# A two-layer graph network on one core: filter taps loaded before x and scaled a part ahead, a rearranged beginning, and other moved steps

## The chip, the cores and the metric

The kernel runs on one core of a Trainium2 chip. A core has a matrix engine (TensorE, PE in the profile, with its weight loads as PEld), a vector engine (VectorE, DVE), an activation engine (ScalarE, ACT), a general engine (GpSimd, POOL) and a queue engine that only issues transfers (SyncE, SP). ACT and POOL issue transfers too. Each engine takes its instructions in the order in which they stand in its own queue, and semaphores order the engines among each other. The metric is the device time of one execution in microseconds, and the median over the runs is compared.

## What is computed

There are 64 graphs of 256 nodes with 256 features each, and an adjacency matrix for each graph, all in float32. Layer 0 is a normalised graph convolution with residual and layer norm; layer 1 has a convolution branch, a message branch and a GRU gate.

```python
# layer 0
deg = adj.sum(-1); d = where(deg != 0, deg, 1) ** -0.5
h = (d[:, :, None] * adj * d[:, None, :] + alpha * eye) @ x
x = layernorm(x + h @ W.T + b)
# layer 1
h = relu(bn1(conv1d(x.T, conv1_w)))             # width 1
h = bn2(conv1d(h, conv2_w, pad=8))              # width 17
x_conv = relu(h + x.T).T
s = x @ w_se.T + b_se                           # 3 columns
A = exp(-(|s_n|^2 + |s_m|^2 - 2 s_n.s_m)) * adj # 256 x 256
x_nmp = A @ relu(x @ w_msg.T + b_msg)
gi = concat(x_conv, x_nmp) @ w_ih.T + b_ih; gh = x @ w_hh.T + b_hh
r, z = sigmoid(gi_r + gh_r), sigmoid(gi_z + gh_z)
x = layernorm(x + (1 - z) * tanh(gi_n + r * gh_n) + z * x)
```

## The kernel before, in words

The graphs go in four quarters of 16 (Q). The convolution of width 17 is done in a frequency domain of 48 points: each graph's hidden rows are transformed by a matrix (`p_dft`, L496), the transforms of a quarter are gathered in the tile `V`, multiplied there with the transformed filter (`p_k`, L559), and transformed back on DVE in small steps (`real_transform`, `complex_begin`, `complex_end`), in place in the same tile, called `VM` or `M`.

**Setup** (L1053 to L1108). Weights, vectors and first graphs are loaded. `tables` (L215) writes cosine rows on one partition (`period`, `fwd_row`, `w_row`) with many small DVE copies and spreads them by transfers into `fwd` and `wt`. `batch_norms` (L165) turns the batch norm vectors into factors: on DVE and POOL, then broadcast over the partitions by six matmuls with diagonal matrices (`p_norm`, L187), then multiplied into the weight tile `wc1` of the first convolution.

**The filter** comes in 13 parts. `load_taps` (L275) loads a part with seven transfers on SP (L291 to L293) into one of two buffers. `weights` (L295) has DVE scale the part (L300), makes 16 matmul records of it (`p_u`, L308), copies them to `u_set` (L311), forms a difference on DVE (L313) and a sum on POOL (L314), and writes three tiles to memory (L316). In the first quarter each of the first 13 graphs has one part beside it.

**A graph** passes through two generators. `layer0(g)` (L353): row sums on ACT (L363), their power on POOL (L373), alpha times the sums on DVE (`adeg`, L375), transposed adjacency and diagonal (L384 to L390), x scaled (L402, ACT), b0 added to x on POOL (L403), `p_hT` (L410), `p_out` (L420), scaling and residual on DVE (L425), then `layernorm` (L319): statistics on DVE, power on POOL (L329), `ln_mr` on DVE (L332), normalising on ACT (L334), and a store. `layer1(g)` (L444): `p_conv` (L457), squares of the three columns on DVE (L467 to L470), `p_msg`, `p_dft`, `p_rows` (L509), `p_dist` with the exponential on ACT (L521), the product with the adjacency on DVE (`aT`, L524), `p_nmp` (L533).

`graphs` (L1021) interleaves them: while graph i is in `layer1`, graph i+2 is in `layer0`, graph i+3 has its sums taken, and the loads of i+3 are issued. `PLACES` (L1012) says after which of the seven pieces of `layer1` a step of `layer0` or of the other work (a filter part in the first quarter) is put. The order inside an engine's queue is made by a planner ahead of the run, which takes ready instructions in the order of the program; `tc.issue_after(op)` makes the instructions in its block that run on op's engine stand behind op. `load` (L104) puts both loads of a graph on SP; the x tile has two buffers, and one comes free when L425 of the graph two before has read it. In `layer0`, the end of the layer norm (`ENDS`, L1029) was put behind the squares and the eviction of `p_conv`.

**Later quarters.** The frequency products run in 12 steps (L1171); in the first quarter each step also takes three pieces of the next graphs (`begin`). After that the GRU (`gru`, L877; `p_g`, L893) of one quarter runs beside the graphs of the next. The last quarter's GRU runs alone, and its last graph ends with the code at L935 to L965.

Of the kernel before, what the change touches and what calls it, by code (L numbers as in the profile page):

```python
# [9 lines left out]
F32 = mybir.dt.float32  # L10
# [16 lines left out]
def kernel(  # L27
# [76 lines left out]
    def load(g):  # L104
        if g >= B:
            return
        ain[g] = loads.tile([P, NCH, N], F32, name="adj_t")
        nc.sync.dma_start(ain[g], adj[g].rearrange("(c p) m -> p c m", p=P))
        xin[g] = loads.tile([P, NCH, D], F32, name="x_t")
        nc.sync.dma_start(xin[g], x[g].rearrange("(c p) f -> p c f", p=P))  # L110

# [15 lines left out]
    nc.scalar.copy(warm, neg_half)  # L127
    for i, a in enumerate((bn1_g, bn2_g, bn1_b, bn2_b, bn1_m, bn2_m, bn1_v, bn2_v)):
        (nc.sync if i % 2 else nc.scalar).dma_start(vectors[2 * i : 2 * i + 2], a.rearrange("(c p) -> c p", p=P))
    nc.scalar.dma_start(w0, w0T.rearrange("(k p) o -> p k o", p=P))  # L130
    load(1)
# [33 lines left out]
    def batch_norms(pool):  # L165
# [10 lines left out]
        nc.vector.tensor_mul(g, g, v)  # L176
        nc.vector.tensor_mul(m, m, g)
        nc.vector.tensor_sub(b, b, m)
        nc.vector.tensor_copy(bn2_bias, b[:, 2:4])

        ones = pool.tile([P, P], F32, name="ones")
        nc.vector.memset(ones, 1.0)
        rows = [bank("p_norm") for _ in range(2)]
        for i, col in enumerate((g[:, 0:1], g[:, 1:2], b[:, 0:1], b[:, 1:2], g[:, 2:3], g[:, 3:4])):
            diagonal = pool.tile([P, P], F32, name="diagonal", bufs=2)
            nc.vector.tensor_scalar(diagonal, ident, col, None, op0=ALU.mult)
            nc.tensor.matmul(rows[i // 4][:, i % 4 * P : (i % 4 + 1) * P], ones, diagonal, start=True, stop=True)  # L187
# [4 lines left out]
        nc.vector.tensor_copy(wc1[0:1, 0, :D], rows[0][0:1, D:])  # L192
# [22 lines left out]
    def tables(pool):  # L215
# [12 lines left out]
        nc.gpsimd.memset(fwd, 0.0)  # L228
        for r in range(2):
            nc.vector.memset(fwd_row[:, :, 2 * r], 1.0)  # L230
# [9 lines left out]
        with tc.issue_after(DIAGONAL[0]):  # L240

            for r in range(2):
                nc.vector.memset(w_row[:, :, r, NF], (0.5, 1.0)[r])
# [7 lines left out]
        for j in range(GT // 2 + 2):  # L251

            first = NT * (j - 1) - PAD
            lo, hi = max(first, 0), min(first + FL, P)
            nc.sync.dma_start(fwd[lo:hi, j, :], fwd_row[:, lo - first : hi - first])

# [16 lines left out]
    TAPS_OF = {}  # L273

    def load_taps(pool, n):  # L275
# [17 lines left out]
        nc.sync.dma_start(tp[KT - 1 :], taps(GC - 1, TR, 1, 1))  # L293

    def weights(pool, n, scale):  # L295
# [4 lines left out]
        nc.vector.tensor_mul(tp, tp, scale[:KT].unsqueeze(1).to_broadcast([KT, ng, D]))  # L300
# [3 lines left out]
        for i in range(2):  # L304
# [7 lines left out]
            if i == 1:  # L312
                nc.vector.tensor_sub(us[3], us[1], us[0])  # L313
                nc.gpsimd.tensor_tensor(us[2], us[0], us[1], op=ALU.add)  # L314
                for d, u in zip(ud, (us[0], us[3], us[2])):
                    nc.gpsimd.dma_start(d[:, n * ng : (n + 1) * ng], u)  # L316
            yield

    def layernorm(y, eps=LN_EPS, normed=None):  # L319

        chunks = range(y.shape[1])
        st = small.tile([P, NCH, nc.vector.BN_STATS_DIM], F32, name="ln_st")
        mv = small.tile([P, NCH, nc.vector.BN_AGGR_DIM], F32, name="ln_mv")
        rs = small.tile([P, NCH], F32, name="ln_rs")
        for c in chunks:
            nc.vector.bn_stats(st[:, c, :], y[:, c, :])
            nc.vector.bn_aggr(mv[:, c, :], st[:, c, :])
        nc.vector.tensor_scalar(rs[:, : len(chunks)], mv[:, : len(chunks), 1], eps, None, op0=ALU.add)  # L328
# [3 lines left out]
        nc.vector.scalar_tensor_tensor(mr[:, : len(chunks)], mv[:, : len(chunks), 0], -1.0, rs[:, : len(chunks)], op0=ALU.mult, op1=ALU.mult)  # L332
# [16 lines left out]
    EVICTED, RELU, SQUARED, AGGREGATED, LAYER0 = {}, {}, {}, {}, {}  # L349
    ADJT, X1, X_SCALED, DIAGONAL = {}, {}, {}, {}  # L350


    def layer0(g):  # L353
# [19 lines left out]
        nc.gpsimd.tensor_tensor(dis, deg, neg_half[:, :NCH], op=ALU.pow)  # L373
        adeg = small.tile([P, NCH], F32, name="adeg")
        nc.vector.tensor_scalar(adeg, deg, alpha_t, None, op0=ALU.mult)  # L375
# [27 lines left out]
        nc.gpsimd.tensor_tensor(x_t, x_t, b0_t.unsqueeze(1).to_broadcast([P, NCH, D]), op=ALU.add)  # L403

        yield
        hT = work.tile([P, DCH, N], F32, name="hT", bufs=1)
# [23 lines left out]
        yield from layernorm(x1, normed=NORMED)  # L430
# [437 lines left out]
    def normed(g, part, y):  # L868

        yield from layernorm(y, 4 * LN_EPS)  # L870
        nc.scalar.dma_start(out[g].rearrange("(c p) d -> p c d", p=P)[:, part], y)
# [5 lines left out]
    def gru(g):  # L877
# [57 lines left out]
        def squashed(c):  # L935
            rz = G[:, c, :, GR : GZ + 1, :].rearrange("p h t d -> p h (t d)")
            nc.scalar.activation(rz, rz, AF.Tanh, scale=0.5)  # L937

        squashed(1)

        def finished(part):
            both = G[:, part].rearrange("p c h t d -> p (c h) t d")
            chunks = both.shape[1] // 2
            r, z, n, i = (both[:, :, j, :] for j in (GR, GZ, GN, GI))
            nc.vector.scalar_tensor_tensor(n, r, 1.0, n, op0=ALU.add, op1=ALU.mult)
            i4 = i.rearrange("p (c h) d -> p c h d", h=2)
            bias = bn_t.rearrange("p (h d) -> p h d", h=2).unsqueeze(1).to_broadcast([P, chunks, 2, HD])
            nc.vector.tensor_tensor(i4, i4, bias, op=ALU.add)
# [10 lines left out]
        if g == B - 1:  # L959
            finished(slice(1, 2))  # L960
            ended()
# [298 lines left out]
```

## Time and profile before

| what | us |
|---|---|
| median of 3 runs (2070.37 to 2078.38) | 2074.39 |
| the profiled execution's own time | 2077.37 |
| its span | 2075.6 |
| PE busy | 1993.8 |
| DVE busy | 1360.7 |
| first `p_conv` | 34.10 |
| transposes of graph 2, of graph 12 (`p_x1T`) | 66.49, 244.27 |
| first frequency products of the first quarter | about 299.9 |
| end of the last matmul | 2064.1 |

The profile is of one execution. A row of the groups or waits names the source line, the engine, and the tiles as output<-input. A wait is written as "who <- whom: total, times, longest". The chain of work is followed back from the last instruction; each row has a start, a duration and the engine with its tile and line. "SPq" is SP's queue. The granted clock is the share of full speed that TensorE had. Times count from the span's start.

### The profile page before, as it was taken

The page shows a single profiled execution, that of the slowest core. Times are in us where ns is not written, and L with a number is a line of the kernel's source. Part 1 is how long each engine was busy: PE and PEld are TensorE (multiplying, and loading weights), DVE is VectorE, ACT ScalarE, POOL GpSimd, SP SyncE. Part 2 cuts the span into 40 slices and gives each one's busy share as a digit, 9 for nine tenths or more (in the row PEclk, how much of TensorE's full clock was granted, in tenths as well). Part 3 has the DMA queues.
Part 4 walks back from the last instruction along what each step waited for, and adds up shares of the span by engine and source line. Part 5 has one row for each costly group of instructions (what it writes and reads, how often), then busy time and mean ns, then how long its engine had stood idle before and what let it go on. Part 6 is the DMA issues. An engine that isn't in the chain of part 4 may idle for free.

```text
span 2075.6 us, 26338 instructions
## 1 busy us (share of the span) xinstructions
PE 1993.8 (96%) x8157; PEld 1445.7 (70%) x8157; DVE 1360.7 (66%) x3192; ACT 972.6 (47%) x2283; POOL 663.4 (32%) x672
## 2 busy tenths in 40 slices
PE   6989999999999999999999999999999999999997
PEld 5877788888667766777777766677767865555554
DVE  5434457587456788764455778775444899977776
ACT  3656664477442234556654223456655223333333
POOL 3433421022432234223332224323232034434442
PEclk9999999999999999999999999999999999999999
DMA  3765656544437655343334664434333944543431
GB/s 103 235 187 173 182 189 221 178 148 159 111 111 220 188 145 148 112 127 105 120 97 154 214 191 128 116 126 138 97 87 92 298 128 124 146 104 99 97 89 58
DMA packets 268936, 298.04 MB, mean 144 GB/s; under 512 B 84192, under 2 KB 211252, under 8 KB 268798
## 3 DMA queue, kind: packets, MB, share of 16 engines
q1 hardware_dynamic: 208846, 200.37, 33.2%
q10 hardware_dynamic: 44480, 67.39, 9.1%
q0 software_dynamic: 15472, 28.61, 6.4%
q8 instruction: 66, 1.08, 0.2%
q14 instruction: 72, 0.59, 0.1%
HBM read 193.19 MB, written 103.06 MB: 143 GB/s over the span
## 4 chain that ended last, share of the span: by engine, by line
PE 75%; DVE 12%; DMA 5%; ACT 3%; issue 2%; SPq 1%; POOL 1%; ACTq 0%; POOLq 0%; DVEq 0%
PE p_g L893 34%; PE p_k L559 10%; PE p_nmp L533 5%; PE p_hT L410 5%; PE p_out L420 4%; PE p_conv L457 4%; PE p_msg L478 3%; PE p_dft L496 3%; PE p_u L308 2%; PE p_dist L520 2%; PE p_x1T L440 1%; DMA u<-ud 1%; DMA taps<-in_conv2T_dram 1%; DMA inputs<-x_d 1%; PE p_adjT L384 1%
## 5 line engine op out<-in xcount | busy, mean ns | idle before, releaser
L893 PE MATMUL p_g<-wall,sums 128*128 128x384 f32 x1536 | 533.8, 488 | 2.8 <-DVE G L918 1.7
L893 PEld LDWEIGHTS p_g<-wall,sums 128*128 128x128 f32 x1536 | 284.9, 190 | 187.9 <-issue 9.5
L893 PE MATMUL p_g<-wall,inputs 128*128 128x384 f32 x1152 | 405.4, 487 | 6.9 <-DVE G L911 6.9
L893 PEld LDWEIGHTS p_g<-wall,inputs 128*128 128x128 f32 x1152 | 216.7, 190 | 157.4 <-DVE G L911 12.8
L864 POOL TENSOR_TENSOR sums<-inputs 128x384 f32<-128x384 f32 x128 | 141.8, 1108 | 332.3 <-PE p_g L893 309.5
L329 POOL TENSOR_TENSOR ln_rs<-ln_rs,neg_half 128x2 f32<-128x2 f32 x129 | 96.5, 748 | 458.7 <-DVE ln_rs L328 331.0
L524 DVE TENSOR_TENSOR aT<-aT,adjT 128x512 f32<-128x512 f32 x64 | 46.1, 720 | 253.5 <-ACT aT L521 253.5
L559 PE MATMUL p_k<-u,VM 128*128 128x256 f32 x736 | 171.3, 383 | 3.7 <-DMA u<-ud 2.4
L403 POOL TENSOR_TENSOR x_t<-x_t,b_t 128x512 f32<-128x512 f32 x64 | 89.1, 1392 | 249.4 <-ACT x L402 178.5
L559 PEld LDWEIGHTS p_k<-u,VM 128*128 128x128 f32 x736 | 139.6, 192 | 26.8 <-ACT ab L605 3.1
L410 PE MATMUL p_hT<-adjT,x 128*128 128x256 f32 x512 | 128.5, 396 | 13.3 <-ACT x L402 11.8
L533 PE MATMUL p_nmp<-aT,msg 128*128 128x256 f32 x512 | 125.3, 389 | 13.8 <-DVE aT L524 13.8
L937 ACT ACTIVATE G<-G 128x512 f32<-128x512 f32 x128 | 80.5, 631 | 123.7 <-DVE G L962 86.4
L334 ACT ACTIVATE x_g<-x_g,ln_mr,ln_rs 128x256 f32<-128x256 f32 x128 | 70.0, 593 | 137.8 <-DVE ln_mr L332 133.5
L420 PE MATMUL p_out<-w,hT 128*128 128x256 f32 x512 | 123.7, 385 | 7.8 <-ACT hT L415 7.6
L457 PE MATMUL p_conv<-wc,xn 128*128 128x259 f32 x512 | 124.6, 385 | 1.1 <-issue 1.1
L478 PE MATMUL p_msg<-wmsg,xn 128*128 128x256 f32 x512 | 121.3, 379 | 0.0
L533 PEld LDWEIGHTS p_nmp<-aT,msg 128*128 128x128 f32 x512 | 98.9, 194 | 30.7 <-DVE aT L524 16.9
L420 PEld LDWEIGHTS p_out<-w,hT 128*128 128x128 f32 x512 | 96.2, 192 | 30.8 <-ACT hT L415 13.8
L410 PEld LDWEIGHTS p_hT<-adjT,x 128*128 128x128 f32 x512 | 93.3, 195 | 34.5 <-ACT x L402 17.9
L864 POOL TENSOR_TENSOR sums<-inputs,sums 128x384 f32<-128x384 f32 x64 | 79.0, 1234 | 116.2 <-PE p_g L893 115.7
L496 PE MATMUL p_dft<-fwd,h 128*128 128x240 f32 x512 | 114.3, 366 | 0.0
(163 smaller groups left out, 3496.3 us busy)
## 6 DMA issues: line engine op xcount, KB each, us to landing
u<-ud SPq DMA_DIRECT2D x284, 256.0 KB
xn_d<-xn ACTq DMA_DIRECT2D x64, 512.0 KB
inputs<-xn_d SPq DMA_DIRECT2D x64, 512.0 KB
ud<-u_set POOLq DMA_DIRECT2D x39, 480.0 KB, 5.4
adj_t<-in_adj_dram SPq DMA_DIRECT2D x64, 256.0 KB
x_t<-in_x_dram SPq DMA_DIRECT2D x64, 256.0 KB
x_d<-x ACTq DMA_DIRECT2D x64, 256.0 KB
xc_d<-VM SPq DMA_DIRECT2D x64, 256.0 KB
```

Of the source, the lines that this page charges most:

```text
L329: nc.gpsimd.tensor_tensor(rs[:, : len(chunks)], rs[:, : len(chunks)], neg_half[:, : len(chunks)], op=ALU.pow)
L403: nc.gpsimd.tensor_tensor(x_t, x_t, b0_t.unsqueeze(1).to_broadcast([P, NCH, D]), op=ALU.add)
L410: nc.tensor.matmul(p[:, k, :], x1[:, mc, k * P : (k + 1) * P], adjT[:, mc, 1 - mc : 3 - mc, :].rearrange("p n q -> p (n q)"), start=mc == ...
L420: nc.tensor.matmul(p[:, c, :], hT[:, k, c * P : (c + 1) * P], w0[:, k, :], start=k == 0, stop=k == DCH - 1)
L457: nc.tensor.matmul(p, x1T[:, k, c * P : (c + 1) * P], wc1[:, k, :], start=k == 0, stop=k == DCH - 1)
L478: nc.tensor.matmul(p[:, c, :], x1T[:, k, c * P : (c + 1) * P], wmsg[:, k, :], start=k == 0, stop=k == DCH - 1)
L496: nc.tensor.matmul(p[:, t0 * FL : t1 * FL], h[:, c, k * P : (k + 1) * P], fwd[:, first : first + t1 - t0, :].rearrange("p t f -> p (t f)") ...
L533: nc.tensor.matmul(p[:, k, :], msg[:, mc, k * P : (k + 1) * P], aT[:, mc].rearrange("p n q -> p (n q)"), start=mc == 0, stop=mc == NCH - 1,)
L559: nc.tensor.matmul(p[:, j * D : (j + 1) * D], v[:, k, :], u[:, k, :], start=k == 0 and j == 0 and not onto, stop=k == DCH - 1, skip_group_ ...
L864: nc.gpsimd.tensor_tensor(S[i], x, y, op=op)
L893: nc.tensor.matmul(p[:, : 3 * HD] if k == 0 else p[:, HD:], a[:, k], wall[:, b, k].rearrange("p t d -> p (t d)"), start=first and k == 0, ...
L937: nc.scalar.activation(rz, rz, AF.Tanh, scale=0.5)
```

## The change

Nothing of what is computed is different. The parts:

- **Filter taps.** In the first quarter a graph's x load is put on SP behind the taps of the next part (before: with the adjacency load, ahead of them). The scaling of a part is done one part ahead, on DVE behind `aT` of the running graph. The difference, the sum and the three writes of a part are put behind `adeg` and the degrees' power of the graph three ahead. Part 0 starts one place later in graph 0.
- **Beginning.** The adjacency of graph 1 is loaded ahead of the batch norm vectors; of those, two are issued by ACT, three by POOL, three by SP. The cosine rows stand behind the second graph's diagonal, the rows for the filter behind the normalised `wc1`; the batch norm is cut in two pieces, whose matmuls come beside graph 1's `p_out`. Its diagonal matrices stand in `VM`. Two biases pass through a small tile.
- **Layer norm of layer 0.** `ln_mr` stands behind `adeg` of the next graph and is a piece of its own; the normalising on ACT waits for the eviction of `p_conv` alone. The b0 addition is a piece later.
- **Transform pieces** in the steps 4 to 11 of the first quarter stand on DVE behind the latest squares, diagonal and `aT` of the graphs.
- **The last graph** of all does the first half of the columns of its first 128 rows early, and takes the statistics of each half by itself.

```diff
+    def load_adj(g):
         ain[g] = loads.tile([P, NCH, N], F32, name="adj_t")
         nc.sync.dma_start(ain[g], adj[g].rearrange("(c p) m -> p c m", p=P))
+    def load_x(g):
         xin[g] = loads.tile([P, NCH, D], F32, name="x_t")
         nc.sync.dma_start(xin[g], x[g].rearrange("(c p) f -> p c f", p=P))
...
+    load_adj(1)
     for i, a in enumerate((bn1_g, bn2_g, bn1_b, bn2_b, bn1_m, bn2_m, bn1_v, bn2_v)):
-        (nc.sync if i % 2 else nc.scalar).dma_start(vectors[2 * i : 2 * i + 2], a.rearrange("(c p) -> c p", p=P))
+        (nc.scalar if i < 2 else nc.gpsimd if i < 5 else nc.sync).dma_start(
+            vectors[2 * i : 2 * i + 2], a.rearrange("(c p) -> c p", p=P)
+        )
+    load_x(1)
     nc.scalar.dma_start(w0, w0T.rearrange("(k p) o -> p k o", p=P))
-    load(1)
...
+        with tc.issue_after(DIAGONAL[1]):
+            nc.vector.tensor_mul(g, g, v)
...
+            for i, col in enumerate((g[:, 0:1], g[:, 1:2], b[:, 0:1], b[:, 1:2], g[:, 2:3], g[:, 3:4])):
+                nc.vector.tensor_scalar(VM[:, i, :P], ident, col, None, op0=ALU.mult)
+        yield
         rows = [bank("p_norm") for _ in range(2)]
...
-        nc.vector.tensor_copy(wc1[0:1, 0, :D], rows[0][0:1, D:])
+        NORMALISED.append(nc.vector.tensor_copy(wc1[0:1, 0, :D], rows[0][0:1, D:]).ins)
...
+        behind_diagonal = ExitStack()
+        behind_diagonal.enter_context(tc.issue_after(DIAGONAL[1]))
         for r in range(2):
             nc.vector.memset(fwd_row[:, :, 2 * r], 1.0)
...
-        with tc.issue_after(DIAGONAL[0]):
+        load_x(2)
+        yield
+        with tc.issue_after(NORMALISED[0]):
             for r in range(2):
                 nc.vector.memset(w_row[:, :, r, NF], (0.5, 1.0)[r])
...
+        TAPS_OF["last"] = nc.sync.dma_start(tp[KT - 1 :], taps(GC - 1, TR, 1, 1)).ins
+    def scaled(tp, scale):
+        nc.vector.tensor_mul(tp, tp, scale[:KT].unsqueeze(1).to_broadcast([KT, GW // NPARTS, D]))
...
-        nc.vector.tensor_mul(tp, tp, scale[:KT].unsqueeze(1).to_broadcast([KT, ng, D]))
+        if n == 0:
+            scaled(tp, scale)
...
+            if i == 1 and n + 1 < NPARTS:
+                with tc.issue_after(WEIGHED[n]):
+                    scaled(TAPS_OF[n + 1], scale)
+            yield
+        with tc.issue_after(ADEG[n + 3]), tc.issue_after(POWERS[n + 3]):
+            nc.vector.tensor_sub(us[3], us[1], us[0])
+            nc.gpsimd.tensor_tensor(us[2], us[0], us[1], op=ALU.add)
+            for d, u in zip(ud, (us[0], us[3], us[2])):
+                nc.gpsimd.dma_start(d[:, n * ng : (n + 1) * ng], u)
+        yield
...
+        with tc.issue_after(ADEG[first]) if first in ADEG else ExitStack():
+            nc.vector.scalar_tensor_tensor(mr[:, : len(chunks)], mv[:, : len(chunks), 0], -1.0, rs[:, : len(chunks)], op0=ALU.mult, op1=ALU.mult)
+        if normed is not None:
+            yield
...
+        yield
+        with tc.issue_after(POWERS[max(g, 1)]):
+            nc.gpsimd.tensor_tensor(x_t, x_t, b0_t.unsqueeze(1).to_broadcast([P, NCH, D]), op=ALU.add)
...
+        top = slice(0, 1)
+        squashed(0, top)
+        y = mixed(top, top)
+        st = small.tile([P, NCH, nc.vector.BN_STATS_DIM], F32, name="ln_st")
+        nc.vector.bn_stats(st[:, 0, :], y[:, 0, :HD])
+        squashed(1)
+        finished(slice(1, 2), mixed(slice(1, 2)))
+        nc.vector.tensor_add(quarter(0, 1), quarter(0, 1), p5)
+        squashed(0, slice(1, 2))
+        mixed(top, slice(1, 2))
+        nc.vector.bn_stats(st[:, 1, :], y[:, 0, HD:])
+        NORMS.append(normed(g, top, y, st))
+        ended()
...
-            load(first + i + 3)
+            if first:
+                load(first + i + 3)
+            else:
+                load_adj(i + 3)
...
-                    with tc.issue_after(EVICTED[first + i]), tc.issue_after(SQUARED[first + i]):
+                    with tc.issue_after(EVICTED[first + i]):
                         run(ENDS.pop())
...
                     next(of_layer0(first + i + 3), "end")
+                    next(given["layer0"], "end")
...
+                if piece == 0 and not first:
+                    with tc.issue_after(TAPS_OF["last"]):
+                        load_x(i + 3)
...
+        run(take(firsts[0], 2))
+        with tc.issue_after(STATISTICS[0]):
+            next(firsts[1])
+            scale2 = next(norms)
+        run(firsts[0])
+        run(fill)
+        next(firsts[1])
+        ENDS[0] = firsts[1]
...
+        others[0] = later(others[0])
...
+                if step >= 4:
+                    with ExitStack() as behind_graphs:
+                        for done in (SQUARED, DIAGONAL, WEIGHED):
+                            behind_graphs.enter_context(tc.issue_after(done[max(done)]))
+                        run(take(real, 1))
+                        run(complex_begin(step))
```

## The prediction

> **What bounds the kernel.** I read the page first, then busy time by stretch, then TensorE's waits, then the chain of work where they fall.
>
> ```profile
> span 2075.6 us, 26338 instructions
> PE 1993.8 (96%) x8157; PEld 1445.7 (70%) x8157; DVE 1360.7 (66%) x3192; ACT 972.6 (47%) x2283; POOL 663.4 (32%) x672
> ```
>
> TensorE (PE) is the bound. The change removes no matmul, so it can win only where PE stands idle (81.8 us in all) or runs at a reduced clock. By stretch (columns: length, busy time of PE, PEld, DVE, ACT, POOL; granted clock; DMA share; GB/s):
>
> ```profile
> 0.00:34.10 34.10, 17.18 (x57) 12.74 (x58) 21.04 (x142) 11.13 (x29) 11.34 (x21) 0.89 0.37 109
> ...
> 66.49:244.27 177.78, 163.47 (x781) 135.48 (x780) 76.62 (x178) 109.14 (x280) 68.97 (x71) 0.96 0.65 193
> ...
> 402.30:412.60 10.30, 8.15 (x25) 5.71 (x26) 4.96 (x9) 5.72 (x13) 1.26 (x1) 0.67 0.08 27
> ...
> 2064.10:2075.60 11.50, 0.01 (x1) 0.00 (x0) 5.50 (x19) 2.66 (x5) 1.32 (x2) 0.67 0.07 23
> ```
>
> Idle PE sits in four places: the beginning (first p_conv at 34.10), graphs 2 to 11 of the first sixteen (66.49 to 244.27), a spot at 402, and the tail after the last matmul. The change edits all four. Single graphs, from one p_x1T to the next:
>
> ```profile
> 99.44:120.26 20.82, 17.67 (x79) 14.27 (x78) 10.15 (x26) 10.84 (x28) 8.20 (x10) 0.89 0.78 224
> ...
> 174.77:193.85 19.08, 15.94 (x79) 13.10 (x78) 8.96 (x22) 10.84 (x28) 7.58 (x9) 1.00 0.65 190
> ...
> 228.60:244.27 15.67, 15.67 (x79) 13.18 (x78) 6.91 (x17) 10.84 (x28) 6.06 (x6) 1.00 0.61 187
> ```
>
> The same work takes 15.67 us when nothing stalls, 19.08 with one stall, 20.82 with a stall and a lowered clock. PE's waits before 300 us (total, times, longest), SP's own wait, and the chain through one stall:
>
> ```profile
> PE p_nmp L533 <- DVE aT L524: 13.0, 4, 3.5
> ...
> PE p_norm L187 <- DVE bn L178: 6.3, 1, 6.3
> ```
>
> ```profile
> SPq L110 <- DVE x L425: 54.4, 12, 11.9
> ```
>
> ```profile
> 101.26 0.39 SPq L110
> ...
> 101.69 2.53 SPq L291
> ...
> 104.26 2.98 SPq L291
> ...
> 107.28 6.25 DMA taps<-in_conv2T_dram
> ...
> 113.70 0.10 DVE taps L300
> ...
> 115.96 0.69 DVE aT L524
> ```
>
> SP holds the x load (L110) until L425 frees its buffer; five of the seven taps issues stand behind it. The taps land at 113.5. DVE has their scaling (L300) ahead of aT (L524), although the exponentials that aT needs were ready at about 112.1. So p_nmp starts at 116.69.
>
> **The change, part by part.** All sums are against the profiled execution: span 2075.6, time 2077.37, so 1.8 lies around the span. The median of the three runs is 2074.39; I take savings off that.
>
> **1. Taps before x, scaled a part ahead.** Nothing is removed: 13 scalings of 1.2 us, 91 issues and 13 sums remain. The x load moves behind the taps. Without it in between, the issues after 101.69 start 2.5 us earlier (99.18, where SP began to wait). The u_set sum and difference with three 480 KB writes move from before p_x1T (DVE 97.03, POOL 96.94) to behind adeg and the degrees' power of the graph three ahead (102.6 and 103.7). So the write burst follows the taps instead of meeting them, and L425 is no longer behind a difference that took 3.37 us. The scaling goes behind aT of the graph before the one that uses it. New wait: DVE may stand at L300 for late taps. Behind it would be L425, the statistics and next graph's squares (L467). With aT begun 12.7 us into a graph (96.42 against 83.76), and taps that even in the stalled graph landed 14.1 us in, less at least 2.5, they are there at about 11.6 or sooner. If that cover is gone, each late us above some 2 of DVE slack falls on p_rows. The x load itself: issued 101.26, first read by L402 at 129.92. A delay of some 4 us is covered. Adjacency and wall loads behind it on SP have a graph's slack as well.
>
> Size: graphs 2 to 11 took 177.78; ten at 15.67 are 156.7; the excess is 21.1. The waits proper are 13.0 + 1.3 (p_u on L300) = 14.3; the rest is clock. The Trainium skill (TensorE: Matmul & The Clock Gate, "What's actually happening") says that PE falls to half clock after an idle window of about 3.4 us. That speaks against counting the rest, since three of the four waits are 3.1 to 3.2. The rows decide: the graph with a 3.15 wait had clock 0.89 and took 1.74 longer than the one with 3.14. By the rule I would save about 14 plus one throttling (2); by the rows 21.1. I take 18.5, leaving 2.6 for denser DMA (193 GB/s becomes some 215; the freest stretch, 83.76 to 99.44, moved 259).
>
> **2. The beginning.** Removed: nothing but waits. Order moved: some 30 fwd_row copies (0.1 to 0.2 each) behind DIAGONAL[1], the w_row pieces (10.96 to 13.25) behind NORMALISED. Before, ACT had graph 1's row sums at 10.1, but DVE took them at 13.18, behind the w_row pieces: 3.1 late. Graph 0's diagonals waited from 7.9 to 10.40 behind the copies. Chain after, by these durations: the first sums 0.5 earlier, since ACT issues two bn loads instead of four and one of them waited 2.2; scaled x(0) at 8.4, p_hT(0) 8.4 to 11.8, p_hT(1) to 14.7 (2.94), p_out(0) to 16.6 (1.74), L425 and statistics to 18.6 (2.0), power 0.71, ln_mr and normalising to 20.8, transposes 0.6, two copies 0.9: first p_conv at 22.6. Meanwhile p_norm (3.12 at half clock, about 1.6 at full) runs after p_out(1) at about 19, and its product into wc1 (0.68 + 0.41) ends by 21.5. I add 1 for DVE beside POOL (L186 took 1.30 there against 0.28 alone): 23.6 instead of 34.1, so 10.5. Ends: 6 if the tables delay L425 and fwd; 12.5.
> The three bn loads on POOL cost 0.6 to 0.8 each (L1062, L1063), about 2, ahead of ident; the first adjacency lands only at 5.1, which covers them; uncovered, 2. The Trainium skill (DMA: Bandwidth & Descriptors, "Issuing engines are not separate DMA queues") says another issuing engine saves only issue time. By it adj_t(1) gains about 1; by the row (issued at 5.40 after a load issued at 1.76 had landed) 3.7. It matters little: graph 1's sums wait for x(0) on ACT anyway. I count only the 0.5. The two bias loads gain two POOL copies, not in the trace: nearest row a 1x256 memset, 0.30; ends 0.1 and 0.8; hidden.
>
> **3. Transform pieces behind the graphs' operations (steps 4 to 11 of the first quarter).**
>
> ```profile
> 402.18 0.33 DVE VM L614
> 402.51 0.08 DVE scols L470
> 402.59 0.07 DVE ln_mr L332
> ...
> 403.19 0.59 ACT x L334
> ...
> 404.86 2.94 PE p_hT L410 x8
> ```
>
> Transform pieces stood between L467 (399.43) and L470; PE lost 2.15 between 402.3 and 404.9, and the stretch's mean clock of 0.67 over 10.3 us means 6.8 us at half clock, costing 3.4: 5.5 in all. From 301.6 to 402.3 PE never waits, so there is nothing else to win. DVE there is busy 66 of 100.7, so pieces deferred have room. I take 4.5; ends 0 and 5.5.
>
> **4. ln_mr behind adeg, normalising a piece later.** Same instruction count. ACT's L334 stops waiting for squares and ln_mr (32.9 us over 30 graphs, on ACT). PE's share later on is 10.8 us of p_hT waiting for L402, which queues behind L334, and 2.4 of p_rows on ln_mr; the first 3.8 or so belong to part 3. Against: ln_mr now stands before the squares, so DVE waits out POOL's power. Between 411 and 515 the power ends 0.2 to 0.6 after the squares began; p_rows is later still on PE, so that is covered. Bounds -2 and 8; I take 3.5. The b0 addition on POOL (1.26 to 1.4) moves one piece later; L425 is 3 us or more behind it.
>
> **5. Tail.** The last matmul ends at 2064.1; then full-width pieces of 0.42 (128x256) and 0.63 run for the last chunk. Half of it is done earlier, with DVE idle between 2058.5 and 2060.3. Six pieces shrink by some 0.15 to 0.2 (1.0), and the second chunk's power no longer stands in front of the last difference (0.5), nor as much DVE work (0.5): 2.0; ends 0.5 and 3.
>
> Sum: 18.5 + 10.5 + 4.5 + 3.5 + 2.0 = 39.0; less 2.5 because graph 0 no longer has p_u as filler in its early pieces and the order shifts elsewhere: 36.5. 2074.4 - 36.5 = **2038**.
>
> **Rivals.** *Stalls only move (0.17):* scaling stands behind aT but taps are still late, and p_rows or p_u waits instead. For: DMA share already 0.65 to 0.85. Against: the 2.5 us and the moved burst. Part 1 gives 5: 2051. *The beginning is bound by loads and tables (0.12):* part 2 gives 3, by the fwd and wt transfers (28.48 to 33.8 for wt) or DVE order: 2045. *Everything works, clock included (0.09):* ends of 1 to 5 taken together (21 + 12.5 + 5.5 + 6 + 3): 2026. *Slower (0.04):* ln_mr blocks DVE in front of the squares wherever POOL's power queues behind the input sums (1.0 to 1.2 each). Over 48 later graphs this outweighs the gain from about 1 us a graph on PE; at 1.2 it costs 58 and gives 2096. In the trace the power ends at most 1.7 after adeg, and mostly 3 to 5 before the squares, so it is unlikely. *Unchanged (0.02).* The likeliest, 2030 to 2046, has the remaining 0.56.
>
> **Numbers.** 0.5% (10.4 us) is about what this kernel's measurement can tell from nothing. Above 2064 only the last two rivals: faster 0.94, same 0.02, slower 0.04. For 8 in 10 the range runs from the full gain to the half-failed part 1 with 3 for spread: 2025 to 2054.
>
> **What would show it.** First p_conv near 23.6; graphs 2 to 11 at 15.7 to 16 each with no p_nmp wait on aT and clock 1.00; no half clock near the first quarter's last steps; ln_mr before the squares; about 9.5 from the last matmul to the end. Wrong if DVE's L300 still waits for taps with PE idle after it, or if p_rows waits for ln_mr in the later graphs.

## The result, and the profile after

The changed kernel takes **2053.26 us** (median of four runs, 2052.44 to 2057.72) beside 2072.38 us for the kernel before on the same chip (2068.34 to 2078.38): a ratio of 0.9907, 95% interval 0.9882 to 0.9933. A later set of runs gave 2055.13 and 0.9935 (0.9922 to 0.9947). It is faster by about 0.9%, and by less than the 36.5 us that were forecast: 19.1 us by these medians and 24.5 between the two profiled executions (2077.37 and 2052.9). The profiled execution of the kernel before, from which the forecast read its savings, is a long one: in five sets of runs the medians of that kernel lie between 2069.05 and 2072.38.

The head of the page after:

```profile
span 2051.1 us, 26391 instructions
PE 1985.3 (97%) x8157; PEld 1441.8 (70%) x8157; DVE 1374.5 (67%) x3199; ACT 961.2 (47%) x2285; POOL 677.9 (33%) x677
```

PE's idle time fell from 81.8 us to 65.8. Its busy time fell as well, from 1993.8 to 1985.3, with the same 8157 matmuls: that part is clock (mean granted clock 0.989 before, 0.993 after). Together they are the 24.5. By stretch (length, busy PE, PEld, DVE, ACT, POOL; clock; DMA share; GB/s): up to the first p_conv, the same ten graphs that took 177.78 before, and the two graphs behind.

```profile
0.00:25.64 25.64, 15.12 (x57) 11.56 (x58) 20.52 (x138) 10.37 (x27) 12.65 (x25) 0.96 0.43 115
58.81:215.49 156.68, 156.68 (x781) 132.06 (x780) 65.48 (x182) 106.17 (x280) 71.77 (x70) 1.00 0.70 217
...
215.49:242.41 26.92, 24.69 (x125) 20.25 (x124) 12.76 (x30) 18.38 (x50) 14.36 (x14) 1.00 0.61 196
```

The ten graphs now run without any idle PE and at full clock, 15.65 us each (one 15.79): all of the 21.1 us is there. What PE waits for between 25 and 2060 us (total, times, longest) has changed. First one line of the kernel before, then the changed kernel:

```profile
PE p_hT L410 <- ACT x L402: 11.8, 15, 1.7
```

```profile
PE p_out L449 <- ACT hT L444: 11.1, 5, 3.2
...
PE p_rows L538 <- DVE scols L499: 7.3, 4, 2.4
...
PE p_hT L439 <- ACT x L431: 3.1, 8, 0.5
```

The 13.0 us of p_nmp on aT in the first quarter are gone, and so are most waits of p_hT for its scaled x; in their place stand waits of p_rows for scols (1.0 us before), and longer ones of p_out for hT (6.9 us before, the longest 1.3).

Where the time went is seen best by stages. The table is worked out from the traces: the start of the first p_conv; then the time from the start of one graph's last p_nmp to that of another's (graphs counted from 0, so that "1 to 11" holds graphs 2 to 11). Each row is one profiled execution; "after, run again" is the changed kernel on another chip, and the rows below it are the experiments told next.

| kernel | first p_conv | 1 to 11 | 11 to 13 | 18 to 19 | 19 to 28 | 28 to 63 |
|---|---|---|---|---|---|---|
| before | 34.10 | 177.78 | 28.30 | 23.21 | 111.00 | 1081.34 |
| after | 25.64 | 156.68 | 30.87 | 19.39 | 114.04 | 1084.10 |
| after, run again | 25.47 | 157.79 | 32.51 | 19.39 | 114.07 | 1084.34 |
| after, part 4 undone | 25.59 | 157.73 | 34.33 | 18.63 | 111.05 | 1078.40 |
| after, adjacency copy first | 25.65 | 156.54 | 31.36 | 18.63 | 111.04 | 1084.33 |
| before, x behind taps | 33.00 | 158.97 | 28.30 | 19.95 | 111.00 | 1082.21 |
| before, scaling ahead | 33.30 | 178.13 | 30.13 | 19.94 | 111.11 | 1082.10 |
| after, old writes | 25.57 | 184.59 | 30.52 | 19.39 | 114.03 | 1084.47 |
| after, old pieces | 25.61 | 156.54 | 30.87 | 19.05 | 113.76 | 1084.73 |
| after, rows late | 27.63 | 156.54 | 30.87 | 19.39 | 114.06 | 1086.35 |
| part 4 undone, old writes | 25.63 | 178.03 | 30.13 | 18.63 | 111.07 | 1078.10 |
| order of loads only | 25.48 | 164.63 | 28.33 | 18.63 | 111.09 | 1080.63 |
| the same, split copies | 23.42 | 158.45 | 28.32 | 18.63 | 111.08 | 1077.97 |
| the same, bias addition moved | 23.40 | 158.45 | 28.31 | 18.63 | 111.06 | 1079.45 |

### The profile page after: what moved, and what is told of

It reads as the page before. It is cut to its first block, busy times and chain, and to the rows that moved or that the text cites. A ratio compares the mean times of both kernels' runs of the same rounds, so it can differ in the third digit from the quotient of the medians.

```text
span 2051.1 us, 26391 instructions
## 1 busy us (share of the span) xinstructions
PE 1985.3 (97%) x8157; PEld 1441.8 (70%) x8157; DVE 1374.5 (67%) x3199; ACT 961.2 (47%) x2285; POOL 677.9 (33%) x677
## 4 chain that ended last, share of the span: by engine, by line
PE 77%; DVE 14%; DMA 3%; ACT 2%; issue 2%; POOL 1%; SPq 0%; POOLq 0%; ACTq 0%; DVEq 0%
PE p_g L922 34%; PE p_k L588 11%; PE p_nmp L562 5%; PE p_out L449 5%; PE p_hT L439 5%; PE p_conv L486 4%; PE p_msg L507 4%; PE p_dft L525 3%; PE p_u L329 2%; PE p_dist L549 2%; PE p_x1T L469 1%; DVE VM L780 1%; DVE ln_st L352 1%; PE p_adjT L413 1%; DMA inputs<-x_d 1%
## 5 line engine op out<-in xcount | busy, mean ns | idle before, releaser
L434 POOL TENSOR_TENSOR x_t<-x_t,b_t 128x512 f32<-128x512 f32 x64 | 100.6, 1572 | 220.6 <-ACT x L431 155.6
L966 ACT ACTIVATE G<-G 128x512 f32<-128x512 f32 (+1 forms) x129 | 80.9, 628 | 126.3 <-DVE G L993 89.1
L486 PEld LDWEIGHTS p_conv<-wc,xn 128*128 128x128 f32 x512 | 98.0, 192 | 23.0 <-issue 1.1
```

The costliest lines, as they stand in the source:

```text
L486: nc.tensor.matmul(p, x1T[:, k, c * P : (c + 1) * P], wc1[:, k, :], start=k == 0, stop=k == DCH - 1)
```

## Experiments

**Which of part 1's three edits takes the stalls away?** The first two runs take the kernel before and add one of them each.

```diff
-            load(first + i + 3)
+            if first:
+                load(first + i + 3)
+            else:
+                load_adj(i + 3)
...
+                if piece == 0 and not first:
+                    with tc.issue_after(TAPS_OF["last"]):
+                        load_x(i + 3)
```

> The kernel before with one edit: in the first sixteen graphs the x load stands behind the taps loads; the scaling stays ahead of aT and the burst of writes where it was. The kernel computes the same. If the order of the loads is the cause of the stalls: graphs 2 to 11 near 15.7 us each, 18 to 21 us faster than before, about 2053. If the scaling's place ahead of aT is: taps come about 2.5 us earlier, waits of 3.2 shrink to under 1, and half or less of the time comes back (5 to 12 us), with p_nmp still waiting for aT. If neither alone will do (the burst of writes meets the taps): under 5 us.

Measured: 2052.86 us, ratio 0.9921 (0.9892 to 0.995). Graph 2 takes 17.27 us, with a wait of p_u for the first taps (1.3); behind it the graphs take 15.67 us each, but for one of 16.34. The order of the loads alone does what part 1 does (18.8 of its 21.1 us). By its ratio this one edit to the kernel before is worth about as much as the whole change (0.9907).

```diff
-        nc.vector.tensor_mul(tp, tp, scale[:KT].unsqueeze(1).to_broadcast([KT, ng, D]))
+        if n == 0:
+            scaled(tp, scale)
...
+                if n + 1 < NPARTS:
+                    with tc.issue_after(WEIGHED[n]):
+                        scaled(TAPS_OF[n + 1], scale)
```

> The kernel before with one edit: each part's taps are scaled behind aT of the part before instead of in front of their own part's aT; loads and writes stay as they were. The kernel computes the same. If the place of the scaling is the cause: 18 to 21 us faster than before, about 2053, and graphs 2 to 11 near 15.7 us each, although the taps still land 14 us into a graph. If the late loads are the cause: VectorE waits for taps at the new place and p_rows or p_u waits behind it, gain under 8 us.

Measured: 2077.06 us, ratio 1.0039 (1.0019 to 1.006): slightly slower than before. Not p_nmp but p_u now waits for the scaled taps, 16.9 us in eleven waits. That is the forecast's rival "stalls only move", with p_u as the one that waits. The next run shows why, and that late taps are not needed for it: the changed kernel, with the sum, the difference and the writes alone back in their old place.

```diff
+            if i == 1:
+                nc.vector.tensor_sub(us[3], us[1], us[0])
+                nc.gpsimd.tensor_tensor(us[2], us[0], us[1], op=ALU.add)
...
-        with tc.issue_after(ADEG[n + 3]), tc.issue_after(POWERS[n + 3]):
-            nc.vector.tensor_sub(us[3], us[1], us[0])
-            nc.gpsimd.tensor_tensor(us[2], us[0], us[1], op=ALU.add)
...
```

> The changed kernel with one edit: the u_set sum and difference and their three writes stand in front of the graph's first transposes again, as before, instead of behind adeg; loads behind taps and scaling ahead stay. The kernel computes the same. If the order of loads alone took the stalls away (the run with only the x load moved says so): graphs 2 to 11 stay at 15.65 each, and graphs 12 and 13, where the squares now take 2.3 us beside GpSimd's 2.97 us sum, get 2.5 us back, so 2 to 3 us faster than the changed kernel, about 2050.5. If the moved burst was needed: waits for taps or aT return, 5 us slower or more.

Measured: 2079.63 us, ratio 1.0052 (1.0032 to 1.0071), so the second expectation; the first, that the order of the loads would be enough here too, failed. VectorE's timeline in one of its graphs, and the line of PE's waits:

```profile
89.90 0.69 DVE L552 TENSOR_TENSOR aT<-aT,adjT 128x512 f32<-128x512 f32 x1 [4.68 <-ACT aT L549]
90.51 3.38 DVE L334 TENSOR_TENSOR u_set<-u_set,u_set 120x1024 f32<-120x1024 f32 x1
93.81 1.21 DVE L313 TENSOR_TENSOR taps<-taps,scale 85x1024 f32<-85x1024 f32 x1
```

```profile
PE p_u L329 <- DVE taps L313: 16.9, 11, 1.6
```

The scaling waits for no transfer. It stands behind the difference, which takes 3.38 us beside GpSimd's sum of 2.38, and PE asks for the taps right behind p_x1T. So the second edit (scaling behind aT) makes the third (difference behind adeg) necessary, while the first needs neither: with the scaling in front of aT, as in the run with x behind the taps, VectorE does it (1.22 us, at 88.48) while it waits for the exponentials anyway, and is then still idle for 4.39. The third edit without the second was not run.

What the third edit costs shows at the end of that part of the work. In a graph with a filter part, p_u keeps PE busy between p_x1T and p_conv, and GpSimd's sum is over when the squares begin (80.08 and 80.36 in one graph). In graph 13 there is no p_u left, and the squares come while the sum still runs. VectorE, GpSimd and PE of the changed kernel there:

```profile
234.86 2.32 DVE L496 SCALAR_TENSOR_TENSOR sq<-scols 128x6 f32<-128x6 f32 x1
...
237.48 2.69 DVE L416 SCALAR_TENSOR_TENSOR adjT<-ident,adeg,adjT 128x128 f32<-128x128 f32 x2
```

```profile
234.18 2.97 POOL L339 TENSOR_TENSOR u_set<-u_set,u_set 120x1024 f32<-120x1024 f32 x1
...
238.74 1.27 POOL L434 TENSOR_TENSOR x_t<-x_t,b_t 128x512 f32<-128x512 f32 x1
```

```profile
240.32 1.53 PE L439 MATMUL p_hT<-adjT,x 128*128 128x256 f32 x6 [1.66 <-DVE adjT L416]
```

The squares, 0.17 us elsewhere, end when the sum does, and p_rows waits 0.56 us. Then GpSimd issues the three writes and does its bias addition (L434, to 240.01). The first of the two diagonals behind the squares ends at 237.83 without delay; the second, begun at 237.75, ends at 240.17, 0.16 behind the bias addition, and p_hT waits 1.66 us for it. So of the 2.6 us between graphs 11 and 13 (30.87 against 28.30) the smaller share is the sum beside the squares, and the larger a diagonal beside the bias addition; why that diagonal, begun 1 us ahead of the addition, did not end before it is not shown. The loss is absent where the writes keep their old place and the scaling too (28.30 to 28.33). The Trainium skill (SBUF — State Buffer, "Who interferes with whom") says that GpSimd and a VectorE operation with both inputs in SBUF take one port pair in turn, the later one waiting out the earlier; for the squares the trace agrees, with an end at 237.18 against the sum's 237.15.

**Part 4.** Undone alone:

```diff
-        with tc.issue_after(ADEG[first]) if first in ADEG else ExitStack():
...
-        if normed is not None:
-            yield
...
-                    with tc.issue_after(EVICTED[first + i]):
+                    with tc.issue_after(EVICTED[first + i]), tc.issue_after(SQUARED[first + i]):
                         run(ENDS.pop())
```

The bias addition went back to its old place as well.

> The changed kernel with its part 4 alone undone: the product ln_mr stands behind the squares again, the normalising step on ScalarE behind both, and the bias addition on GpSimd where it was. The kernel computes the same. Theory A (part 4 costs time: the normalising step now stands ahead of the adjacency copy on ScalarE and waits there for ln_mr, and ln_mr stands ahead of the squares on VectorE and waits there for GpSimd's power): 3 to 6 us faster than the changed kernel, so 2047 to 2050; the waits of 2.2 us at 913 and 1408 and the waits of 0.2 to 0.8 us for the adjacency copy go, and the waits of p_hT for the normalised x come back. The forecast's theory (part 4 gains 3.5): 3.5 us slower, about 2057. Rival (the later graphs shift only because other work falls elsewhere against loads and clock windows): within 1 us of 2053.

Measured: 2047.34 us, ratio 0.9905 (0.9876 to 0.9934). By its ratio it is no better than the changed kernel (0.9907), so the medians don't decide. The stages do: 3.0 us less from graph 19 to 28 and 5.7 less from 28 to 63, while graphs 5 and 13 happened to lose 4.5 (most of it in graph 13, where p_hT waited 1.71 us and two half-clock windows followed). So part 4 does not gain 3.5 us; in these stages it costs about 8.7. Two runs on one chip, further down, show it by their medians too. ScalarE in the changed kernel, what PE makes of it, and ScalarE with part 4 undone, behind the same graph's p_nmp:

```profile
414.59 1.09 ACT L363 ACTIVATE x<-x,ln_mr,ln_rs 128x256 f32<-128x256 f32 x2 [1.93 <-DVE ln_mr L359]
415.59 0.56 ACT L414 COPY adjT<-p_adjT 128x512 f32<-128x512 f32 x1
```

```profile
416.21 0.44 PE L538 MATMUL p_rows<-ident,scols 128*128 128x128 f32 x2 [0.24 <-ACT adjT L414]
```

```profile
415.57 0.58 ACT L411 COPY adjT<-p_adjT 128x512 f32<-128x512 f32 x1
417.12 1.09 ACT L360 ACTIVATE x<-x,ln_mr,ln_rs 128x256 f32<-128x256 f32 x2 [0.96 <-DVE ln_mr L358]
```

With part 4 undone, as in the kernel before, the wait for the squares keeps the normalising step behind the adjacency copy. Without that condition it stands in front, waits 1.93 us for ln_mr, and the copy, the diagonals, p_rows (0.24) and p_hT (0.53) start late. The next run moves only this back:

```diff
-                    with tc.issue_after(EVICTED[first + i]):
-                        run(ENDS.pop())
...
+                if piece == APPLIED:
+                    done = COPIED.get(first + i + 2, EVICTED[first + i])
+                    with tc.issue_after(EVICTED[first + i]), tc.issue_after(done):
+                        run(last)
```

> The changed kernel with one move: on ScalarE the normalising step of a graph stands behind the adjacency copy of the graph two ahead instead of in front of it; ln_mr stays behind adeg. The kernel computes the same. If the loss of part 4 is ScalarE's order (theory A, first half): 3 to 5 us faster than the changed kernel, about 2049, and the small waits of the diagonals for the adjacency copy go. If it is VectorE's (ln_mr in front of the squares waits for GpSimd's power): within 1 us of the changed kernel, and the waits of 2.2 us at 913 and 1408 stay. If the normalising step comes too late for p_hT this way: slower, with p_hT waiting for x 20 times or more.

Measured: 2049.53 us, ratio 0.9916 (0.9891 to 0.994). Graphs 19 to 28 are back at 111.04, so those 3.0 us are ScalarE's order. From graph 28 to 63 nothing changed (1084.33): ScalarE's order is not the cause there, and what is left of part 4 is VectorE's order and the bias addition, which the last run below clears. All six profiled executions in which ln_mr need not stand behind the squares lie between 1084.1 and 1086.4 in that stage, all eight in which it must between 1078.0 and 1082.2. One such place in the changed kernel (VectorE, then PE):

```profile
915.14 0.16 DVE L359 SCALAR_TENSOR_TENSOR ln_mr<-ln_mv,ln_rs 128x2 f32<-128x2 f32 x1 [1.67 <-POOL ln_rs L355]
...
915.50 0.17 DVE L499 TENSOR_SCALAR scols<-nsq 128x4 f32<-128x4 f32 x1
```

```profile
915.81 0.41 PE L538 MATMUL p_rows<-ident,scols 128*128 128x128 f32 x2 [2.18 <-DVE scols L499]
```

GpSimd had a sum of inputs, another layer norm's power and the degrees' power to do first. The squares themselves were done at 913.2, but the last operation of that chain, scols, came behind ln_mr, and p_rows waited 2.18 us. With part 4 undone scols comes first: p_rows waits 0.48 us, and p_hT behind it 1.13 for its scaled x.

**Part 3 undone.**

```diff
-                run(merge(products(step), take(real, 1 if q else 0)))
-                if q:
-                    run(complex_begin(step))
+                run(merge(products(step), take(real, 1)))
+                run(complex_begin(step))
```

> The changed kernel with part 3 undone: the transform pieces of the first quarter's steps 4 to 11 stand where they were. The kernel computes the same. If part 3 took the stall at 402 away: the stretch from graph 18 to 19 grows from 19.4 to 23.2 us, and the gap of 1.79 us in front of p_nmp at 381 goes, net 2 to 4 us slower, about 2056. If that stall came only with the phase of the kernel before (with only the x load moved, and with only the scaling moved, the same stretch took 19.95 with the pieces at their old place): within 1 us of the changed kernel.

Measured: 2053.86 us (two runs), ratio 0.9926 (0.9906 to 0.9946): no difference. The second expectation holds: the stall of 5.5 us at 402 stands in the one trace of the kernel before alone; in the three runs with the pieces at their old place and some other edit, the stage took 19.05 to 19.95. Part 3 only seemed to give its 3.8.

**The beginning.** First the copies of the table behind the first graph's statistics:

```diff
-        behind_diagonal.enter_context(tc.issue_after(DIAGONAL[1]))
+        behind_diagonal.enter_context(tc.issue_after(STATISTICS[0]))
...
-        fill = tables(setup)
-        next(fill)
         for stage in firsts:
             next(stage)
         run(take(firsts[0], 2))
+        fill = tables(setup)
+        next(fill)
```

> The changed kernel with one edit: the copies into fwd_row in the beginning stand behind the first graph's statistics, and no longer behind its first two diagonals. The kernel computes the same. If copies beside GpSimd's work made the first eviction (L454) late: it starts near 16.1 instead of 18.33 and the first p_conv near 23.4 instead of 25.64, 2.2 us faster than the changed kernel. If the chain behind it (norm's product into wc1, end of the first layer norm) or the fwd transfer sets it instead: first p_conv within 0.7 of 25.64, and p_dft waits.

Measured: 2057.86 us (two runs), ratio 0.9945 (0.9925 to 0.9965). The eviction did start at 16.19 instead of 18.33, as the first expectation said, and yet the first p_conv came 2.0 us later, which neither expectation had. The copies now stood in front of ln_mr, while VectorE had nothing to do from 11.7 to 16.2. In the changed kernel (VectorE, then GpSimd):

```profile
12.39 1.20 DVE L250 COPY fwd_row<-period 1x48 f32<-1x48 f32 x1
13.51 1.31 DVE L249 COPY fwd_row<-period 1x48 f32<-1x48 f32 x1
...
18.33 0.47 DVE L454 SCALAR_TENSOR_TENSOR x<-p_out,dis,x_t 128x256 f32<-128x256 f32 x1
```

```profile
12.35 1.19 POOL L153 TENSOR_TENSOR wc<-wc,top 128x518 f32<-128x518 f32 x1 [2.17 <-DMA top<-in_w_seT_dram]
13.50 1.26 POOL L434 TENSOR_TENSOR x_t<-x_t,b_t 128x512 f32<-128x512 f32 x1
```

Copies of 0.19 us take about as long as the addition beside them. Three of them, one behind the other, last 3.95 us, and the 20 behind these hold up an eviction whose p_out ended at 15.95. The remedy is to give VectorE half of the copies ahead of that eviction and half behind ln_mr; it was run on top of the combination below.

**Putting it together.** Part 4 undone, part 1 cut to the order of the loads (scaling in front of its own part's aT, difference, sum and writes as before), parts 2, 3 and 5 kept; beside it the same with the split copies, and the changed kernel again.

```diff
-        if n == 0:
-            scaled(tp, scale)
+        scaled(tp, scale)
...
```

> The changed kernel with part 4 undone and part 1 reduced to the order of the loads: x behind the taps stays, the scaling goes back in front of its own part's aT, the u_set difference, sum and writes go back in front of the first transposes. Parts 2, 3 and 5 stay. The kernel computes the same. If the order of loads is all that part 1 needs and the halves are separate: graphs 2 to 11 at 15.66 each with no wait for taps, graph 12 to 13 at 28.3 instead of 30.9, graphs 19 to 63 as with part 4 undone, so 2040 to 2042, 11 to 13 us faster than the changed kernel. If the later graphs behave as in the run where only the x load was moved (waits that fall on other clock windows): about 2046. If the old places of scaling and difference bring stalls back here: 2053 or more.

```diff
+            if n == SPLIT:
+                behind_diagonal.close()
+                yield
+                behind_diagonal.enter_context(tc.issue_after(PRODUCTS[0]))
...
```

> The run with the order of loads only, and one further edit in the beginning: the last 16 of the 30 copies into fwd_row stand behind the first graph's ln_mr, so that VectorE is free for that graph's eviction and statistics when its p_out ends. The kernel computes the same. If VectorE's sum of work in front of ln_mr(0) sets the first p_conv (copies that take 1.2 to 1.4 us each beside GpSimd's additions, and 19 more behind them): first p_conv at 22.6 to 23.2 instead of 25.64, 2 to 3 us faster than with the order of loads only. If the fwd transfers, now some 3 us later, hold p_dft: first p_conv early, p_dft waits, net under 1 us. If p_norm or its product into wc1 sets it: first p_conv within 0.7 of 25.6.

> The changed kernel itself, on the same chip as the two runs beside it, as the measure for them: 2051 to 2056.

Measured on one chip: 2046.7 us (0.9883, 0.9868 to 0.9898), **2042.97 us** (0.9874, 0.9861 to 0.9888), and 2055.13 for the changed kernel (0.9935, 0.9922 to 0.9947). Both are faster than the changed kernel, with intervals that do not touch its own. The first missed 2040 to 2042: its profiled execution lost 6.2 us in graph 4, where ScalarE stood still for 4.91 us, which the profile puts down to the taps transfer, and its one write (x_d) went out at the end of that, at 104.37:

```profile
104.79 0.60 ACT L506 ACTIVATE msg<-p_msg 128x512 f32<-128x512 f32 x1 [4.91 <-DMA taps<-in_conv2T_dram]
```

No other profiled execution has that. It may be the price of leaving the write burst beside the taps, which the changed kernel's third edit avoids, but that is not shown: the two later runs have the burst at the same place and no such stop. The split copies bring the first p_conv to 23.42 (22.6 to 23.2 was expected). The intervals of the two ratios overlap, so these 2 us are shown by the stage and not by the medians.

An earlier attempt undid part 4 and the writes together but left the scaling behind aT:

> The changed kernel with part 4 undone and the u_set sum, difference and writes at their old place. The kernel computes the same. With part 4 undone alone the later graphs (19 to 63) took 9.7 us less, and graphs 5 and 13 lost 4.5 to the writes behind adeg. If the two are separate: this one keeps the 9.7 and gives the 4.5 and the 2.6 of graph 13 back, 11 to 13 us faster than the changed kernel, 2040 to 2042. If the loss of graph 13 comes from elsewhere or comes back later: 2046 to 2048, as with part 4 undone alone.

Measured: 2070.81 us, ratio 1.0005 (0.999 to 1.002). The gain of part 4 undone was kept (111.07 and 1078.10), and the whole 21 us of part 1 lost (178.03), by the same eleven waits of p_u as above. This run differs from the one with old writes (2079.63 us, ratio 1.0052, 1.0032 to 1.0071), made on the same chip, in part 4 alone: 8.8 us by the medians, with intervals apart. So the cost of part 4 shows there too.

The last run puts half of part 4 back into the fastest kernel: the bias addition one piece later.

```diff
-        if g > 1:
-            nc.gpsimd.tensor_tensor(x_t, x_t, b0_t.unsqueeze(1).to_broadcast([P, NCH, D]), op=ALU.add)
         yield
...
+        with tc.issue_after(POWERS[max(g, 1)]):
+            nc.gpsimd.tensor_tensor(x_t, x_t, b0_t.unsqueeze(1).to_broadcast([P, NCH, D]), op=ALU.add)
```

> The run with the order of loads only and the split copies, with one half of part 4 put back in: the bias addition on GpSimd stands one piece later, as in the changed kernel; ln_mr and the normalising step stay behind the squares. The kernel computes the same. If the loss of part 4 is all in ln_mr and the normalising step: within 2 us of the run without it (2043), and graphs 19 to 63 as there. If the later addition (1.26 us in GpSimd's queue, in front of the input sums) is a share of the loss: 3 to 6 us slower, about 2047, with p_out waiting longer for hT in the later graphs.

Measured: 2042.59 us, ratio 0.9873 (0.9853 to 0.9893), as without it, and the later stages are within 1.5 us. The bias addition's place is worth next to nothing; part 4's loss is in ln_mr and the normalising step.

## Why the prediction was right and wrong

The direction was right, and the time inside the wide range, but 2053 lies outside the 2030 to 2046 of the case held likeliest. That it lies inside 2025 to 2054 is in part luck: the upper end was set by a half-failed part 1 (2051), and part 1 gave all of its gain. What brought the time there was part 4, with the wrong sign, graph 13, and smaller shortfalls of parts 2, 3 and 5. Some 3 us more come from reading the savings off one long execution: the 24.5 us, taken off 2074.4 as the forecast did, would give 2050. Between the two profiled executions, by the forecast's own terms:

| term | forecast | measured | cause |
|---|---|---|---|
| 1, graphs 2 to 11 | 18.5 | 21.1 | the rows' value, not the rule's |
| 1, graphs 12 and 13 | 0 | -2.6 | GpSimd's sum beside the squares, its bias addition beside a diagonal |
| 2, first p_conv | 10.5 | 8.5 | copies beside GpSimd |
| graphs 0 and 1 | -2.5 | -0.8 | |
| graphs 14 to 18 | 0 | -0.7 | copy behind the normalising step (118.38 with the copy first) |
| 3 | 4.5 | 3.8 | came without part 3 too |
| 4, graphs 20 to 63 | 3.5 | -5.8 | wrong sign; against the run with part 4 undone it is -8.7 |
| 5, with the last matmuls | 2.0 | 0.9 | |
| sum | 36.5 | 24.4 | |

**Part 1: right in size, wrong in what does it.** The forecast weighed a rule (half clock only after some 3.4 us idle, so 16 us) against the rows (21.1) and took 18.5, leaving 2.6 for denser DMA. The rows were right: 14.3 us of idle PE, and 6.8 us by which the same 781 matmuls kept PE busy longer (163.47 against 156.68, with two half-clock stretches of 6.83 us among them), make 21.1, and the denser DMA (217 GB/s) cost nothing. But the forecast laid the gain on three edits. One does it (18.8 us alone); of the other two, the second loses by itself and needs the third. What it gave as the price of the new place, a wait of VectorE for late taps, never came; the price was GpSimd's work beside VectorE's in graph 13, which it put at nothing.

**Part 4: the step that failed.** The forecast said that L334 "stops waiting for squares and ln_mr" and counted the wait as gain. It named the scaled x behind L334 on ScalarE, but not the adjacency copy, which the condition had kept in front of it; freed, L334 went in front and waited there for ln_mr instead. It did ask what stands behind ln_mr on VectorE, and called that covered because p_rows was later still between 411 and 515. That held there (graphs 19 to 28 are mended by ScalarE's order alone) and not after the first quarter, where GpSimd also has the input sums. The trace of the kernel before had the place (VectorE):

```profile
944.30 0.95 DVE L332 SCALAR_TENSOR_TENSOR ln_mr<-ln_mv,ln_rs 128x2 f32<-128x2 f32 x1 [1.18 <-POOL ln_rs L329]
```

There the power ended 2.06 us after the squares began, and so again at 1434; "mostly 3 to 5 before the squares" passed over it, since scols was done before ln_mr then. So the mechanism of the rival "slower" was there, in a few graphs and at some 5 us, not in every later graph and at 58.

**Part 2: the chain was right, one term too small.** The forecast allowed 1 us for VectorE beside GpSimd and put the first p_conv at 23.6. Three copies took 3.4 us longer than alone, and 20 more stood between them and the eviction. With half of the copies out of the way the first p_conv came at 23.42.

**Part 3** was read from one execution: a stall that no other arrangement shows. **Part 5**: the pieces did shrink, but the last difference (2044.37) still stands behind the second chunk's ln_mr, which waits 0.44 us for GpSimd's power; 10.7 us from the last matmul to the end, not 9.5. The sum of the best ends took 6 for part 4 where its own bound was 8; with it that rival is 2024, not 2026.

## What to carry to other kernels

When a wait is taken from an instruction, ask what that wait kept it behind: an in-order engine that no longer waits in one place may wait in a worse one. Before three edits are made for one stall, try each alone, and look at the last stage in which they are in force, where the work that kept their price apart has run out. A spot where one profiled execution loses time is a cause only if it comes back when something else in the kernel is moved.

## What the runs showed of the hardware

**TensorE's clock is decided window by window.** In all fourteen profiled executions the granted clock changes only on a grid of 3.413 us, the same through the whole execution. Take each such window between 30 and 2030 us that ran at full clock, with PE's idle time in it: of some 8030 windows with less than 1.45 us idle none was followed by half clock, of 64 with 1.45 to 2.0 us eleven were, and of 34 with more than 2.0 us all were. The two bounds were set by looking at these same windows. A window idle from end to end, as in the rule that the forecast weighed, was not needed. Half clock then lasted one to three windows, and each costs up to 1.7 us (half of 3.41). So one wait of 2.2 us costs that much more, or nothing, by where it falls. The same wait at 907 in the run with the adjacency copy first, and at 913 in the changed kernel:

```profile
906.98:910.39 3.41, 1.23 (x6) 0.82 (x6) 1.41 (x6) 1.53 (x3) 1.65 (x3) 1.00 0.69 137
910.39:913.80 3.41, 3.41 (x8) 2.02 (x7) 0.00 (x0) 3.28 (x9) 2.42 (x2) 0.50 0.38 99
```

```profile
910.89:914.30 3.41, 2.74 (x14) 2.16 (x12) 2.58 (x14) 0.82 (x2) 3.27 (x5) 1.00 1.11 316
914.30:917.72 3.42, 1.91 (x8) 1.27 (x9) 1.39 (x5) 2.38 (x6) 0.81 (x2) 1.00 0.66 131
```

In the first it lies in one window, with 2.18 us idle, and the next runs at 0.50; in the second it is cut into 0.67 and 1.51. Waits between the two bounds may go either way: in the run with old writes five windows hold one wait of 1.56 us on p_u each, and three of them were followed by half clock. This would explain why the kernel with old writes and part 4 undone, with eleven waits of this size, ran between 2061.89 and 2075.59 us, and why the kernel before varies from run to run; it is argued from the windows and not shown, since only one execution of each kernel has a trace.

**Short VectorE operations beside a GpSimd addition** ended with that addition, or close to it: 0.19 us became 1.2 to 1.44, and 0.17 became 2.32. A cost read from an operation alone can be too small where GpSimd is at work.
